# Attention and experts on one core: base loads, a square on GpSimd, and a start by halves

## The chip, the core and the metric

The kernel runs on one core of a Trainium2 chip. A core has four computing engines that run side by side and meet only at semaphores: TensorE (PE in the profile; its weight loads are PEld), VectorE (DVE), ScalarE (ACT) and GpSimd (POOL). SyncE (SP) issues transfers; ScalarE and GpSimd can issue them too. Each engine takes its instructions from a list of its own, in the order of that list. TensorE writes its results to PSUM, from which VectorE and ScalarE take them to SBUF.

The metric is the device time of one execution in microseconds (us): lower is better. Before the change the median of three runs is 3160.34 us, from 3158.16 to 3162.79.

## The reference

The input x is [8, 1024, 512]: 8 batches of 1024 tokens. One layer of attention is followed by one layer of experts, each on a layer norm of its input and with its input added back.

```python
# attention, per head of dh = 32 (16 heads)
theta_q = xh / (1 + |w_q|) + b_q + t * phi_q      # t: position; k alike, v without t
Q = concat(cos(theta_q), sin(theta_q)); K alike; V = cos(theta_v) + sin(theta_v)
out = softmax(causal(Q K^T / sqrt(2 dh))) V
theta_out = out / (1 + |w_out|) + b_out
x = x + cos(theta_out) + sin(theta_out)           # sin, cos by a table of 2048 with interpolation
# experts, E = 8, top 2, at most 160 tokens of a batch for an expert
p = softmax(layernorm(x) @ Wr + br); two best experts of a token, place by order of arrival
y = relu(tokens @ W1 + b1) @ W2 + b2; x = x + sum of p * y over the token's experts that kept it
```

## The kernel before

**Attention.** Work goes in 32 iterations n = 4 b + c: batch b, and a chunk c of four heads. An iteration has two pairs of heads. `scores` makes tiles of Q K^T on TensorE (L688, with the mask by L702) in one of three PSUM tiles (`two_banks`), and ScalarE takes each by an exponential (L708); `attend` multiplies the exponentials with v on TensorE (L722), and VectorE takes the result out of one of two PSUM banks (L730). `turn` transposes it back to tokens (L216) and divides by the sums (L757, L759).

Angles are integers whose wrap-around is the turn. For q and k an iteration adds, on VectorE, the transposed x and a base (the position's part of the angle) in `qk_pre` (L529), and takes the remainder by a shift in `angle` (L442). Interpolation is a polynomial in the low 16 bits: `square` (L446, ScalarE) makes (f / 65536 - 0.5)^2 out of them, `sine` (L449) the sine, and `times` (L452, VectorE) multiplies the two. Eight transfers then spread the features to two `qk` tiles (L613). `o_pre` and `o_post` do the same with the attention's output: bias and angle, then square and sine, then L452 on tile `t_r`, the sum with x (L662) and batch statistics (L665).

Bases of chunks 0 to 3 are made once by `make_base` and stored to DRAM (L501); from n = 4 on `load_base` fetches that of iteration n + 2 as one transfer of 1 MB (L509) into a single buffer, free once L529 of the iteration before has read it.

**The router.** When a batch is complete, its router runs between the next batch's attention. At c = 0 of the next batch (in the text `begin` is set there), the last chunk's output is squared and finished (L1924 and L1925) and the router starts: it is a generator that is advanced at fixed places. Its first step, at c = 1, aggregates the statistics, takes inverse roots and makes rows 0 and 1 of the normalised x (L814, two row buffers); each row tile is stored to DRAM for the experts (L820). TensorE transposes rows (L216) and multiplies them with Wr (L876). At the end of c = 3 slot and token numbers are ready (L978, L983).

Then `scatter` writes them to a slot table in DRAM: 16 indirect transfers by GpSimd per batch (L773), each of which waits for the landing of the one before, since they write the same table. `fetch_slots` (L1006, two transfers by GpSimd) reads the table of a batch back; its place in the text is two batches after that batch. Batches 6 and 7 are scattered in `ending`, beside the first expert.

**The order.** TensorE, ScalarE, VectorE and SP issue their instructions in the order of the text (`manual_schedule`). GpSimd is not in that list: the framework's scheduler places its instructions, by dependencies and its own idea of when they are ready.

**The start.** x of batch 0 is loaded by tiles; statistics (`first_stats`), inverse roots and normalisation (`layernorm_first`, tiles by turns on VectorE and ScalarE), and `qk_first` makes the features of n = 0 by halves of 512 tokens. GpSimd makes the positions (L188), the affine part of two bases (L473) and, ahead of that, the constant columns of two v tiles (L381, L382). ScalarE rounds the base (L483, L486), VectorE scales it (L489).

**The experts** follow with nearly two thirds of the time (L1258, L1372, L1491, L1540) and are not changed.

Of the kernel before, what the change touches and what calls it, by code (L numbers as in the profile page):

```python
# [12 lines left out]
F32 = mybir.dt.float32  # L13
I32 = mybir.dt.int32
U16 = mybir.dt.uint16
BF16 = mybir.dt.bfloat16
AF = mybir.ActivationFunctionType
# [5 lines left out]
P = 128  # L23
# [51 lines left out]
def preln_attn_moe_kernel(  # L75
# [133 lines left out]
    def two_banks():  # L209
        return ps_sc.tile([P, 2, 512], F32, name="ps_s")  # L210
# [7 lines left out]
    def magnitude(t):  # L218

        nc.vector.scalar_tensor_tensor(t, t, -1.0, t, ALU.mult, ALU.max)  # L220
        nc.vector.scalar_tensor_tensor(t, t, 1.0, t, ALU.add, ALU.max)
        nc.vector.reciprocal(t, t)

    def in_units(t):

        nc.vector.scalar_tensor_tensor(t, t, UNITS, t, ALU.mult, ALU.max)
# [9 lines left out]
    def first_stats(t0, t1):  # L236
        for t in range(t0, t1):
            st = small.tile([P, nc.vector.BN_STATS_DIM], F32, name="st")
            nc.vector.bn_stats(st, first_tiles[t])
            nc.vector.bn_aggr(first_mv[:, t, :], st)  # L240
# [15 lines left out]
    nc.tensor.transpose(ps, vec_in, ident[: 6 * NCH, : 6 * NCH])  # L256
    nc.vector.tensor_copy(vecs, ps)

    nc.vector.tensor_copy(inv_qk, vecs[:, : 2 * NCH])
    magnitude(inv_qk)  # L260
    in_units(inv_qk)

    ones = own.tile([P, P], F32, name="ones")
    nc.gpsimd.memset(ones, 1.0)

# [26 lines left out]
    def mask():  # L292
        for part in range(2):
            for a in range(2):
                r = slice(a * 64, (a + 1) * 64)
                nc.gpsimd.tensor_copy(later_b[r, part, :], later[r, 1 + part - a, :])
                nc.gpsimd.tensor_copy(keys_b[r, part, part * 64 : part * 64 + 64], ident[r, r])
# [75 lines left out]
            nc.vector.scalar_tensor_tensor(y, t, 1.5, y, ALU.add, ALU.mult)  # L373
        return y

    v_tiles = []
    for i in range(2):
        vt = vp.tile([P, NTT, HPC, 2 * DH], F32, name=f"v_{i}", tag=f"v_{i}")


        nc.gpsimd.memset(vt[:, :, :, DH:], 0.0)  # L381
        nc.gpsimd.memset(vt[:, :, :, DH : DH + 1], 1.0 / (SUM_UNIT * UNITS))  # L382
        v_tiles.append(vt)

    def load_b1():
        t = own.tile([E * NHC, P], F32, name="vec_in")
# [36 lines left out]
    def layernorm_first():  # L423

        mv = first_mv
        rstd = inverse_root(mv[:, :, 1], "rstd")
        off = small.tile([P, NTT], F32, name="top")
        nc.vector.scalar_tensor_tensor(off, mv[:, :, 0], -1.0, rstd, ALU.mult, ALU.mult)
        for t, xt in enumerate(first_tiles):
            if t % 2:  # L430
                nc.scalar.activation(
                    xt, xt, AF.Identity, bias=off[:, t : t + 1], scale=rstd[:, t : t + 1]
                )
            else:
                nc.vector.tensor_scalar(
                    xt, xt, mv[:, t, 0:1], rstd[:, t : t + 1], ALU.subtract, ALU.mult
                )

    def angle(p, r):
        nc.vector.tensor_scalar(r, p, TURN_SHIFT, None, ALU.logical_shift_left)  # L442

    def square(p):
        f = p.bitcast(U16).rearrange("p (s two) -> p s two", two=2)[:, :, 0]
        nc.scalar.activation(p.bitcast(F32), f, AF.Square, bias=split_c, scale=1.0 / FINE)  # L446

    def sine(r):
        nc.scalar.activation(r.bitcast(F32), r, AF.Sin, scale=STEP_ACT)  # L449
# [7 lines left out]
    def make_base(c):  # L457


        p = (base_first, room[0])[c] if c < 2 else (  # L460
            qkt.tile([P, 2, S], F32, name="qk_base") if c == 2 else room[0]
        )
        r = qkt.tile([P, 2, S], I32, name="qk_r").bitcast(F32) if c == 2 else room[1]
        if c > 1:
            nc.gpsimd.iota(
                p, pattern=[[0, 2], [1, S]], base=0, channel_multiplier=0,
                allow_small_or_imprecise_dtypes=True,
            )
        affine = nc.gpsimd.tensor_scalar if c < 2 else nc.vector.tensor_scalar
        for i in range(2):  # L470
            phi = vecs[:, (4 + i) * NCH + c : (4 + i) * NCH + c + 1]
            bias = vecs[:, (2 + i) * NCH + c : (2 + i) * NCH + c + 1]
            affine(p[:, i, :], p[:, i, :], phi, bias, ALU.mult, ALU.add)  # L473
        if c < 2:
            rs = [r[:, i, :] for i in range(2)]
            if c == 1:

                rs = [
                    ep.tile([P, 2, 512], F32, name="e_512", bufs=8).rearrange("p a n -> p (a n)")
                    for _ in range(2)  # L480
                ]
            for i in range(2):
                nc.scalar.activation(  # L483
                    rs[i], p[:, i, :], AF.Identity, bias=round_c[:, :1], scale=UNITS
                )
                nc.scalar.activation(rs[i], rs[i], AF.Identity, bias=round_c[:, 1:])  # L486
                yield
            for i in range(2):
                nc.vector.scalar_tensor_tensor(  # L489
                    p[:, i, :], p[:, i, :], UNITS, rs[i], ALU.mult, ALU.subtract  # L490
                )
        else:
            nc.vector.tensor_scalar(p, p, UNITS, None, ALU.mult)
            if c == 2:
                yield
                nc.vector.tensor_scalar(r, p, ROUNDT, ROUNDT, ALU.add, ALU.subtract)
                yield
                nc.vector.tensor_tensor(p, p, r, ALU.subtract)
            else:
                wrap(p, r)  # L500
        nc.sync.dma_start(base_d[c], p)  # L501
        bases[c] = p

    def load_base(n):
        if n < NCH:
# [26 lines left out]
                )  # L532
            yield p, r

    def qk_first():


        base = bases.pop(0)
        f, r = (qkt.tile([P, 2, S], I32, name=name) for name in ("qk_f", "qk_r"))
        c = qkt.tile([P, 2, S], F32, name="qk_c")  # L540
        pairs = [qkp.tile([P, 2, S], F32, name="qk") for _ in range(2)]
        halves = [slice(h * 512, (h + 1) * 512) for h in range(2)]
        for h, hs in enumerate(halves):
            ps = two_banks()
            for t in range(4):
                by_halves(ps[:, :, t * 64 : (t + 1) * 64], xn_tiles[0][h][:, t, :P])
            for i in range(2):
                for a in range(2):
                    cols = lambda t: t[:, i, hs].rearrange("p (t a q) -> p t a q", a=2, q=64)[
                        :, :, a, :  # L550
                    ]
                    nc.vector.scalar_tensor_tensor(
                        cols(f), ps[:, a, :256].rearrange("p (t q) -> p t q", q=64),
                        inv_qk[:, i * NCH : i * NCH + 1], cols(base), ALU.mult, ALU.add,
                    )
            angle(f[:, :, hs], r[:, :, hs])
        for hs in halves:
            nc.scalar.activation(c[:, :, hs], r[:, :, hs], AF.Abs)
            nc.scalar.activation(
                c[:, :, hs], c[:, :, hs], AF.Sin, bias=quarter_c, scale=-STEP_ACT  # L560
            )
            for i in range(2):
                square(f[:, i, hs])
            sine(r[:, :, hs])
        v = v_pre(0)
        next(v)
        for hs in halves:
            for i, t in enumerate((c, r.bitcast(F32))):
                times(t[:, :, hs], f[:, :, hs], t[:, :, hs])
                send = (nc.sync, nc.gpsimd)[i].dma_start  # L570
                for pr in range(2):
                    for a in range(2):
                        src = slice((2 * pr + a) * DH, (2 * pr + a + 1) * DH)
                        dst = slice(a * 64 + i * DH, a * 64 + (i + 1) * DH)
                        send(pairs[pr][dst, :, hs], t[src, :, hs])
            v_st = rest(v) or v_st
        return pairs, v_st


# [160 lines left out]
    def rest(gen):  # L740
        got = None
        for got in gen:
            pass
        return got
# [1027 lines left out]
    next(base1)  # L1772
    rest_of_loads()
    mask()
    first_stats(2, NTT)
    layernorm_first()
    rest(base0)
    next(base1)
    pairs, v_st = qk_first()
    sine(v_st[1])  # L1780
    square(v_st[0])
    load_x(1)
# [7 lines left out]
    for n in range(NCK):  # L1790
# [36 lines left out]
            turn(0, halves0, pos)  # L1827
        if more:
            angle(*qk_st)
        if begin or c == 3 and b > 0:  # L1830
            next(route)
        if n and n + 2 < NCK:
            load_base(n + 2)
        if n == 2:
            load_mid(b)
        if late:
# [43 lines left out]
        if late:  # L1880
            turn(1, halves1, pos)
            o_st = o_pre(n - 1, pos)
        if begin:
            square(v_st[0])
        rest(choice)
# [4 lines left out]
        if c == 3 and b > 0:  # L1890
            next(route)
            if b > 1:
                fetch_slots(b - 2)
            if b < B - 1:
                scatter()


        some(3, *products)
# [22 lines left out]
        some(3, *ahead)  # L1921
        begin = c == 0 and late
        if begin or not more:
            square(o_st[0])  # L1924
            rest(o_post(n - 1, o_st))  # L1925
        if begin:
            route = router(b - 1)
# [77 lines left out]
```

## Time and profile before

| | before |
|---|---|
| median of the runs | 3160.34 us |
| profiled execution | 3160.96 us |
| its span, first to last instruction | 3159.2 us |
| busy TensorE, VectorE, ScalarE, GpSimd | 3085.4, 2393.9, 1686.1, 421.3 us |
| scatters (L773) on GpSimd | 128, busy 153.6 us, 280.9 us between them until the one before has landed |
| squares of the output (L446 on `o_p`) | 32, median 1.146 us |
| base loads (L509) | 28, 1 MB, 6.5 us to landing |
| row stores (L820) | 72, 256 KB, 2.4 us to landing |
| VectorE's wait for row stores before L814, 190 to 1240 us | 12.8 us in 10 waits |

A row of the timeline has the start in us from the span's begin, the length in us, the engine, the line, the operation, the tile written and the tiles read (`out<-in`), their shapes, how many equal instructions are put together (x8) and, in brackets, how long the engine stood idle before it and what ended that. An engine with a q is its sequencer: SPq rows are issues of transfers. A group's row has busy time and the mean of one in ns, and then the idle time before its instructions. Busy shares are means over stages, and TensorE's instructions are pipelined with modelled ends.

### The profile page before, as it was taken

How to read it: one execution, taken by the hardware profiler on the slowest of the kernel's cores; microseconds unless marked ns; L12 is line 12 of the kernel's file. 1: busy time of each engine (PE TensorE's matmuls, PEld its weight loads, DVE VectorE, ACT ScalarE, POOL GpSimd, SP SyncE). 2: the span in 40 equal slices, each digit the busy share in tenths (PEclk: the TensorE clock that was granted, in tenths of full speed). 3: DMA queues.
4: the chain of work that ended last, by engine and by line, in shares of the span. 5: the costliest groups of instructions: out<-in, count | busy, mean ns of one | idle time of the engine just before them, and what ended most of it. 6: DMA issues, size and time to landing. Idle time of an engine off the chain costs nothing.

```text
span 3159.2 us, 53457 instructions
## 1 busy us (share of the span) xinstructions
PE 3085.4 (98%) x20422; PEld 2149.6 (68%) x20422; DVE 2393.9 (76%) x4962; ACT 1686.1 (53%) x2672; POOL 421.3 (13%) x387
## 2 busy tenths in 40 slices
PE   5999999999999999999999999999999999999998
PEld 2454444544444544689699699699698698698697
DVE  8888888888888776738678678677777777777775
ACT  7888888888788885413423423423423423423423
POOL 3000202010101122320110110010110010110110
PEclk9999999999999999999999999999999999999999
DMA  5435454544545352433523523523523523423421
GB/s 168 148 101 167 110 165 133 156 135 147 155 140 161 81 168 63 142 84 96 156 52 92 156 50 99 155 50 99 150 54 102 142 57 105 135 57 108 133 46 22
DMA packets 288559, 358.86 MB, mean 114 GB/s; under 512 B 28376, under 2 KB 199088, under 8 KB 276272
## 3 DMA queue, kind: packets, MB, share of 16 engines
q1 hardware_dynamic: 264944, 312.20, 33.4%
q0 software_dynamic: 22912, 43.22, 7.5%
q8 instruction: 162, 2.65, 0.4%
q14 instruction: 93, 0.76, 0.1%
q10 hardware_dynamic: 448, 0.02, 0.0%
HBM read 207.02 MB, written 81.22 MB: 91 GB/s over the span
## 4 chain that ended last, share of the span: by engine, by line
PE 75%; ACT 12%; DVE 7%; DMA 3%; issue 2%; SPq 0%; POOLq 0%; POOL 0%; ACTq 0%; DVEq 0%
PE ps_p L1258 30%; PE ps_p L1491 13%; PE ps_s L688 8%; PE ps_p L1372 8%; PE ps_p L1540 7%; PE av L722 7%; ACT e L708 6%; ACT qk_c L598 1%; DMA xn_d<-xn 1%; ACT t_r L449 1%; PE ps_s L216 1%; ACT qk_r L449 1%; ACT L598 1%; DMA qk<-qk_r 1%; ACT L1908 1%
## 5 line engine op out<-in xcount | busy, mean ns | idle before, releaser
L688 PE MATMUL ps_s<-qk 64*128 64x512 f32 (+3 forms) x3072 | 584.6, 503 | 31.3 <-ACT e L708 13.7
L708 ACT ACTIVATE e<-ps_s 128x1024 f32<-128x1024 f32 (+1 forms) x640 | 554.4, 944 | 73.4 <-PE ps_s L702 45.3
L722 PE MATMUL av<-e,v 128*64 128x512 f32 (+3 forms) x3072 | 509.5, 488 | 0.0
L688 PEld LDWEIGHTS ps_s<-qk 64*128 64x128 f32 x3072 | 261.1, 188 | 219.1 <-ACT e L708 105.9
L722 PEld LDWEIGHTS av<-e,v 128*64 128x64 f32 x3072 | 206.0, 137 | 278.9 <-issue 258.5
L1258 PE MATMUL ps_p<-xe,w 128*128 128x256 f32 (+1 forms) x1024 | 317.6, 433 | 1.1 <-issue 1.1
L1258 PE MATMUL ps_p<-xe_s,t 128*128 128x256 f32 (+1 forms) x1024 | 317.7, 433 | 0.0
L1258 PE MATMUL ps_p<-xe,t 128*128 128x256 f32 (+1 forms) x1024 | 317.7, 433 | 0.0
L1336 POOL DMA_INDIRECT out_dram<-y,slots x80 | 127.6, 1595 | 1237.2 <-ACT y L1331 956.8
L773 POOL DMA_INDIRECT slot_d<-token,slot x128 | 153.6, 1200 | 1026.2 <-issue 627.2
L1258 PEld LDWEIGHTS ps_p<-xe_s,t 128*128 128x128 f32 x1024 | 194.4, 190 | 81.4 <-issue 0.8
L1258 PEld LDWEIGHTS ps_p<-xe,t 128*128 128x128 f32 x1024 | 194.2, 190 | 80.4 <-issue 0.4
L1258 PEld LDWEIGHTS ps_p<-xe,w 128*128 128x128 f32 x1024 | 193.7, 190 | 79.4 <-issue 1.2
L1301 DVE TENSOR_TENSOR hid<-hid 128x256 f32<-128x256 f32 (+1 forms) x128 | 63.5, 496 | 199.3 <-ACT hid L1299 199.1
L1258 PE MATMUL ps_p<-xe_s,w 128*128 128x256 f32 (+1 forms) x512 | 158.9, 433 | 0.6 <-ACT p L1274 0.6
L1372 PE MATMUL ps_p<-w,hid 128*128 128x256 f32 x640 | 142.9, 379 | 0.0
L1491 PE MATMUL ps_p<-w,hid 128*128 128x128 f32 x1104 | 141.8, 275 | 0.0
L702 PEld LDWEIGHTS <-keys_b 64*128 64x128 bf16 x1536 | 78.7, 95 | 91.1 <-issue 72.4
L730 DVE TENSOR_SCALAR av_sb<-av,inv_o 128x512 f32<-128x512 f32 x128 | 94.4, 746 | 57.7 <-PE av L722 57.6
L1491 PEld LDWEIGHTS ps_p<-w,hid 128*128 128x128 f32 x1104 | 135.3, 192 | 1.9
L1372 PEld LDWEIGHTS ps_p<-w,hid 128*128 128x128 f32 x640 | 121.1, 190 | 16.4
L1268 ACT COPY hid<-ps_p 128x256 f32<-128x256 f32 (+1 forms) x128 | 53.9, 421 | 139.4 <-PE ps_p L1258 127.4
(314 smaller groups left out, 5502.3 us busy)
## 6 DMA issues: line engine op xcount, KB each, us to landing
w<-in_L_ffn_W_dram SPq DMA_DIRECT2D x256, 256.0 KB, 3.5
w<-in_L_ffn_W_dram SPq DMA_DIRECT2D x64, 512.0 KB, 6.6
qk<-qk_c SPq DMA_DIRECT2D x124, 256.0 KB, 4.6
qk<-qk_r SPq DMA_DIRECT2D x120, 256.0 KB, 5.2
qk_base<-base_d SPq DMA_DIRECT2D x28, 1024.0 KB, 6.5
xn_d<-xn SPq DMA_DIRECT2D x72, 256.0 KB, 2.4
rows_d<-xg SPq DMA_DIRECT2D x70, 256.0 KB, 2.1
x_mid<-in_L_attn_x_dram SPq DMA_DIRECT2D x16, 1024.0 KB, 9.9
```

Source lines behind the costliest of these rows:

```text
L688: nc.tensor.matmul(ps[:, a, at : at + w], lhsT=pair[r, 1, kb * P : (kb + 1) * P], rhs=pair[r, 0, q0 : q0 + w], start=at == 0, stop=not own ...
L702: nc.tensor.matmul(out_, lhsT=keys_b[r, part, :], rhs=late, start=False, stop=part == 1, skip_group_check=True,)
L708: nc.scalar.activation(e, ps[:, :, :n], AF.Exp, scale=UNIT * UNIT / math.sqrt(2 * DH))
L722: nc.tensor.matmul(av[a * 64 : (a + 1) * 64, q0 - 512 * h :], lhsT=vt[:, kb, 2 * pr + a, :], rhs=es[i][:, a, at : at + w], start=kb == 0, ...
L730: nc.vector.tensor_scalar(av_sb, av, inv_o[:, q : q + 1], None, ALU.mult)
L773: queued = nc.gpsimd.indirect_dma_start(out=slot_d[b], out_offset=bass.IndirectOffsetOnAxis(ap=idx, axis=0), in_=src, in_offset=None,)
L1258: nc.tensor.matmul(ps, lhsT=weights[:, k, :], rhs=rows[:, k, :], start=first and k == 0, stop=last and k == 1, skip_group_check=True,)
L1301: TT(g1, g3, h22, ALU.add)
L1336: ins = nc.gpsimd.indirect_dma_start(out=out, out_offset=bass.IndirectOffsetOnAxis(ap=meta[:, e, jj[r], 0:1], axis=0), in_=y, in_offset=No ...
L1372: nc.tensor.matmul(ps, lhsT=hid[:, k, part, cols], rhs=ws[weight][:, k, :], start=first and k == 0, stop=last and k == NHQ - 1, skip_group ...
L1491: nc.tensor.matmul(ps, lhsT=left[:, k, :], rhs=right[:, k, :], start=first and k == 0, stop=k == 3, skip_group_check=True,)
L1540: nc.tensor.matmul(of(ps, b), lhsT=hid[:, k, part, b * P : (b + 1) * P], rhs=ws[weight][:, k, :], start=first and k == 0, stop=last and k ...
```

## The change

1. In an iteration, `load_base` is called ahead of the router's step instead of behind it. On SP this puts seven base loads (n = 5, 9, ..., 29) ahead of the two row tiles' stores.
2. At c = 0 (n = 4, 8, ..., 28) the square of the batch's last output chunk is `square_beside`, called right after `o_pre`: two GpSimd operations, a scale and shift from the 16-bit view, and a product of the tile with itself. The ScalarE `square` of these seven is left out. `scatter()` is called behind it, where before it was called at the end of c = 3. At n = 4 there is nothing to scatter.
3. The start: the v columns are filled behind the masks; the inverse of 1 + |w| for q and k (`inv_qk`, five small VectorE operations) is taken behind the first statistics; VectorE normalises tiles 0 to 4 and ScalarE 5 to 7; the base of chunk 0 is scaled by halves of positions; both, and the features, go half by half in `qk_first`. The store of base 0 comes behind the features' transfers, and v's first product behind the first half's features.

TensorE's list is the same, VectorE's the same but for the start, and ScalarE's the same but for the seven squares and one normalisation.

```diff
@@ -255,10 +255,6 @@
     ps = two_banks()[:, 0, : 6 * NCH]
     nc.tensor.transpose(ps, vec_in, ident[: 6 * NCH, : 6 * NCH])
     nc.vector.tensor_copy(vecs, ps)
-
-    nc.vector.tensor_copy(inv_qk, vecs[:, : 2 * NCH])
-    magnitude(inv_qk)
-    in_units(inv_qk)
     ones = own.tile([P, P], F32, name="ones")
     nc.gpsimd.memset(ones, 1.0)
@@ -373,14 +369,14 @@
             nc.vector.scalar_tensor_tensor(y, t, 1.5, y, ALU.add, ALU.mult)
         return y
-    v_tiles = []
-    for i in range(2):
-        vt = vp.tile([P, NTT, HPC, 2 * DH], F32, name=f"v_{i}", tag=f"v_{i}")
-
-
-        nc.gpsimd.memset(vt[:, :, :, DH:], 0.0)
-        nc.gpsimd.memset(vt[:, :, :, DH : DH + 1], 1.0 / (SUM_UNIT * UNITS))
-        v_tiles.append(vt)
+    v_tiles = [
+        vp.tile([P, NTT, HPC, 2 * DH], F32, name=f"v_{i}", tag=f"v_{i}") for i in range(2)
+    ]
+
+    def v_columns():
+        for vt in v_tiles:
+            nc.gpsimd.memset(vt[:, :, :, DH:], 0.0)
+            nc.gpsimd.memset(vt[:, :, :, DH : DH + 1], 1.0 / (SUM_UNIT * UNITS))
     def load_b1():
         t = own.tile([E * NHC, P], F32, name="vec_in")
@@ -426,17 +422,22 @@
         rstd = inverse_root(mv[:, :, 1], "rstd")
         off = small.tile([P, NTT], F32, name="top")
         nc.vector.scalar_tensor_tensor(off, mv[:, :, 0], -1.0, rstd, ALU.mult, ALU.mult)
-        for t, xt in enumerate(first_tiles):
-            if t % 2:
-                nc.scalar.activation(
-                    xt, xt, AF.Identity, bias=off[:, t : t + 1], scale=rstd[:, t : t + 1]
-                )
-            else:
-                nc.vector.tensor_scalar(
-                    xt, xt, mv[:, t, 0:1], rstd[:, t : t + 1], ALU.subtract, ALU.mult
-                )
-
-
+
+        def by_vector(t):
+            nc.vector.tensor_scalar(
+                first_tiles[t], first_tiles[t], mv[:, t, 0:1], rstd[:, t : t + 1],
+                ALU.subtract, ALU.mult,
+            )
+
+        for t in range(4):
+            by_vector(t)
+        for t in range(5, NTT):
+            nc.scalar.activation(
+                first_tiles[t], first_tiles[t], AF.Identity, bias=off[:, t : t + 1],
+                scale=rstd[:, t : t + 1],
+            )
+        yield
+        by_vector(4)
     def angle(p, r):
         nc.vector.tensor_scalar(r, p, TURN_SHIFT, None, ALU.logical_shift_left)
@@ -444,6 +445,12 @@
     def square(p):
         f = p.bitcast(U16).rearrange("p (s two) -> p s two", two=2)[:, :, 0]
         nc.scalar.activation(p.bitcast(F32), f, AF.Square, bias=split_c, scale=1.0 / FINE)
+
+    def square_beside(p):
+        f = p.bitcast(U16).rearrange("p (s two) -> p s two", two=2)[:, :, 0]
+        t = p.bitcast(F32)
+        nc.gpsimd.tensor_scalar(t, f, 1.0 / FINE, -0.5, ALU.mult, ALU.add)
+        nc.gpsimd.tensor_tensor(t, t, t, ALU.mult)
     def sine(r):
         nc.scalar.activation(r.bitcast(F32), r, AF.Sin, scale=STEP_ACT)
@@ -466,6 +473,7 @@
                 p, pattern=[[0, 2], [1, S]], base=0, channel_multiplier=0,
                 allow_small_or_imprecise_dtypes=True,
             )
+        bases[c] = p
         affine = nc.gpsimd.tensor_scalar if c < 2 else nc.vector.tensor_scalar
         for i in range(2):
             phi = vecs[:, (4 + i) * NCH + c : (4 + i) * NCH + c + 1]
@@ -485,7 +493,14 @@
                 )
                 nc.scalar.activation(rs[i], rs[i], AF.Identity, bias=round_c[:, 1:])
                 yield
-            for i in range(2):
+            if c == 0:
+                for h in range(2):
+                    hs = slice(h * 512, (h + 1) * 512)
+                    nc.vector.scalar_tensor_tensor(
+                        p[:, :, hs], p[:, :, hs], UNITS, r[:, :, hs], ALU.mult, ALU.subtract
+                    )
+                    yield
+            for i in range(2 if c else 0):
                 nc.vector.scalar_tensor_tensor(
                     p[:, i, :], p[:, i, :], UNITS, rs[i], ALU.mult, ALU.subtract
                 )
@@ -499,7 +514,6 @@
             else:
                 wrap(p, r)
         nc.sync.dma_start(base_d[c], p)
-        bases[c] = p
     def load_base(n):
         if n < NCH:
@@ -532,8 +546,9 @@
                 )
             yield p, r
-    def qk_first():
-
+    def qk_first(base0, base1):
+
+        normal = layernorm_first()
         base = bases.pop(0)
         f, r = (qkt.tile([P, 2, S], I32, name=name) for name in ("qk_f", "qk_r"))
@@ -541,6 +556,10 @@
         pairs = [qkp.tile([P, 2, S], F32, name="qk") for _ in range(2)]
         halves = [slice(h * 512, (h + 1) * 512) for h in range(2)]
         for h, hs in enumerate(halves):
+            next(normal, None)
+            next(base0)
+            if not h:
+                next(base1)
             ps = two_banks()
             for t in range(4):
                 by_halves(ps[:, :, t * 64 : (t + 1) * 64], xn_tiles[0][h][:, t, :P])
@@ -563,7 +582,6 @@
                 square(f[:, i, hs])
             sine(r[:, :, hs])
         v = v_pre(0)
-        next(v)
         for hs in halves:
             for i, t in enumerate((c, r.bitcast(F32))):
                 times(t[:, :, hs], f[:, :, hs], t[:, :, hs])
@@ -574,6 +592,7 @@
                         dst = slice(a * 64 + i * DH, a * 64 + (i + 1) * DH)
                         send(pairs[pr][dst, :, hs], t[src, :, hs])
             v_st = rest(v) or v_st
+        rest(base0)
         return pairs, v_st
@@ -1772,11 +1791,12 @@
     next(base1)
     rest_of_loads()
     mask()
+    v_columns()
     first_stats(2, NTT)
-    layernorm_first()
-    rest(base0)
-    next(base1)
-    pairs, v_st = qk_first()
+    nc.vector.tensor_copy(inv_qk, vecs[:, : 2 * NCH])
+    magnitude(inv_qk)
+    in_units(inv_qk)
+    pairs, v_st = qk_first(base0, base1)
     sine(v_st[1])
     square(v_st[0])
     load_x(1)
@@ -1827,10 +1847,10 @@
             turn(0, halves0, pos)
         if more:
             angle(*qk_st)
+        if n and n + 2 < NCK:
+            load_base(n + 2)
         if begin or c == 3 and b > 0:
             next(route)
-        if n and n + 2 < NCK:
-            load_base(n + 2)
         if n == 2:
             load_mid(b)
         if late:
@@ -1880,6 +1900,9 @@
         if late:
             turn(1, halves1, pos)
             o_st = o_pre(n - 1, pos)
+            if c == 0:
+                square_beside(o_st[0])
+                scatter()
         if begin:
             square(v_st[0])
         rest(choice)
@@ -1891,8 +1914,6 @@
             next(route)
             if b > 1:
                 fetch_slots(b - 2)
-            if b < B - 1:
-                scatter()
         some(3, *products)
@@ -1921,7 +1942,8 @@
         some(3, *ahead)
         begin = c == 0 and late
         if begin or not more:
-            square(o_st[0])
+            if not begin:
+                square(o_st[0])
             rest(o_post(n - 1, o_st))
         if begin:
             route = router(b - 1)
```

## The prediction

> **What bounds the kernel now.** First the page's busy shares: TensorE is the bound, in attention (the first 15 slices) as much as in the experts.
>
> ```profile
> PE 3085.4 (98%) x20422; PEld 2149.6 (68%) x20422; DVE 2393.9 (76%) x4962; ACT 1686.1 (53%) x2672; POOL 421.3 (13%) x387
> PE   5999999999999999999999999999999999999998
> ```
>
> So a gain must come out of TensorE's few waits, and anything that keeps TensorE waiting is lost whole. The view of waits, TensorE alone, lists them: behind the start, 13.7 us for ScalarE's exponentials (L708), 4.0 for VectorE's `lg` (L881), 2.6 for the router's rows (L814).
>
> Then I read one begin, that of n = 8 (c = 0), engine by engine in the timeline. GpSimd, from the scatters of batch 0 on (start, length, what):
>
> ```profile
> 317.53 2.97 POOL L773 DMA_INDIRECT slot_d<-token,slot  x1 [264.53 <-issue]
> ...
> 358.44 0.96 POOL L773 DMA_INDIRECT slot_d<-token,slot  x1 [2.87 <-DMA slot_d<-token,slot]
> ...
> 371.52 0.96 POOL L773 DMA_INDIRECT slot_d<-token,slot  x1 [1.42 <-DMA slot_d<-token,slot]
> 373.90 1.57 POOL L1006 DMA_DIRECT2D slots<-slot_d  x2 [1.43 <-DMA slot_d<-token,slot]
> 375.47 0.20 POOL L980 IOTA token<- 128x16 int32 x1
> ```
>
> Each of the 16 scatters waits for the landing of the one before, so they hold GpSimd's queue for 56 us. Behind them stands L1006, which the text issues three iterations later, at n = 11: GpSimd's list is not in the order of the text. VectorE around the same begin:
>
> ```profile
> 351.20 0.69 DVE L442 TENSOR_SCALAR t_r<-o_p 128x1024 int32<-128x1024 int32 x1
> ...
> 355.33 2.28 DVE L452 SCALAR_TENSOR_TENSOR qk_r<-qk_f,qk_r 128x2048 f32<-128x2048 f32 x1
> 358.97 1.23 DVE L452 SCALAR_TENSOR_TENSOR t_r<-o_p,t_r 128x1024 f32<-128x1024 f32 x1 [1.36 <-ACT o_p L446]
> ...
> 364.31 2.72 DVE L529 SCALAR_TENSOR_TENSOR qk_f<-ps_s,inv_qk,qk_base 128x512 int32<-128x512 f32 x4 [1.18 <-PE ps_s L216]
> ...
> 372.42 1.00 DVE L814 TENSOR_SCALAR xn<-x_mid,mv,rstd 128x512 f32<-128x512 f32 x2
> ```
>
> The square is what L452 on `t_r` waits for; its input is ready at 351.9. From L529 to the rows (L814) VectorE has no gap. And TensorE:
>
> ```profile
> 365.11 7.96 PE L722 MATMUL av<-e,v 128*64 128x512 f32 x48
> 373.00 1.13 PE L688 MATMUL ps_s<-qk 64*128 64x512 f32 x4
> 373.97 0.25 PE L702 MATMUL ps_s<-later_b,keys_b 64*128 64x64 bf16 x4
> 374.05 0.67 PE L216 MATMUL ps_s<-ident,xn 64*128 64x64 f32 x16
> ```
>
> At 374.05 it transposes the router's rows, 0.63 us after L814 has made them: VectorE has next to no lead here.
>
> **The change part by part.** *The square by GpSimd.* Seven ScalarE squares of 1.15 us go (L446, n = 4, 8, ..., 28). Each holds back an exponential for which TensorE waits 0.45 us: at most 3.2 us in all. In their place come seven pairs on GpSimd. What the pairs stand behind is read from the built program of the changed kernel, by GpSimd's list (lines of the changed file):
>
> ```
> 43 L452 TensorScalarPtr o_p<-o_p 128x1024
> 44 L453 TensorTensor o_p<-o_p 128x1024
> 45 L792 DMACopy slot_d_62<-token,slot 3328x2 x16
> 46 L1025 DMACopy slots<-slot_d_62 128x8x2
> 47 L1025 DMACopy slots<-slot_d_62 32x8x2
> 48 L999 Iota token 128x16
> 49 L452 TensorScalarPtr o_p<-o_p 128x1024
> ```
>
> The first pair is n = 4's, with no scatters pending. The next is n = 8's, and the 16 scatters of batch 0, their two fetches and an iota stand ahead of it. The text puts them behind, but the scatters' inputs are ready at 316.7 (slot and token, before the end of n = 7), the square's at 351.9, and the list has them in that order for all six batches 0 to 5. The first scatter's wait names the same VectorE instruction as before, so they still start near 317.5. VectorE's order around it is unchanged: L452 on `t_r` waits for GpSimd, and everything behind it waits too: batch statistics, the next features (L529), the rows, all evictions of attention (L730).
>
> How late is it? From the start of the fetches to VectorE: fetches 1.57, iota 0.20, first operation 1.19 (row of L473, the same size), second operation, and 0.3 for hand-overs. The second has two inputs; nearest is L1233, 256 elements:
>
> ```profile
> L1233 POOL TENSOR_TENSOR t<-w,t 128x256 f32<-128x256 f32 x12 | 10.0, 833 | 0.4
> L473 POOL TENSOR_SCALAR qk_base<-qk_base,vecs 128x1024 f32<-128x1024 f32 x2 | 2.4, 1197 | 0.6 <-DVE vecs L257 0.6
> ```
>
> Bounds are 0.83 us (no growth with size) and 3.3 (four times). I take 3.0: the row less 0.1 of fixed cost (L193's smallest memset is 0.09), times four. That makes 6.3 us in all. The Trainium skill (GPSIMD Engine Reference, section 3.1 Elementwise) has 4497 ns for 2048 elements; an estimate from it, half of that, is 2.25 us, and the sum would be 4.5 us smaller.
>
> The fetches start at 373.90, 529.42, 679.04, 826.87, 992.07 and 1132.32 in the six batches. In four of them the last scatters collide with the router's row stores (issued 523.76, 674.90, 825.18, 981.31), which will come later than they; at the undisturbed 2.38 us from issue to the next step, the fetches start at 373.9, 526.1, 676.7, 826.2, 986.0 and 1132.3. L452 on `t_r` starts now at 358.97, 509.73, 660.88, 811.15, 967.22 and 1116.97. With 6.3 added it is late by 21.2, 22.7, 22.1, 21.4, 25.1 and 21.6: sum 134.
>
> What covers it? TensorE goes on with the transposes of L529's input, two attends (L722) and one score tile, and stops at 374.05 for rows that come 21 us late. Cover is the 1.18 us that VectorE waits before L529 and the 0.63 of lead: 1.8 each. Stall: 134 - 11 = **123 us**. After it, TensorE is the bound again and nothing gives the time back.
>
> TensorE also slows after idling. It waits 3.7 us up to 62.18; then:
>
> ```profile
> 34.00:62.00 28.00, 24.28 (x164) 12.96 (x164) 23.83 (x25) 24.71 (x24) 5.83 (x6) 0.99 0.59 199
> 62.00:70.00 8.00, 7.82 (x26) 3.96 (x28) 5.48 (x6) 5.65 (x8) 0.00 (x0) 0.61 0.99 230
> ...
> 836.00:840.00 4.00, 4.00 (x34) 1.25 (x32) 1.08 (x4) 2.05 (x2) 0.00 (x0) 0.57 0.06 25
> ```
>
> (columns: stretch, length, busy of PE, PEld, DVE, ACT, POOL, granted clock, DMA share, GB/s). A mean of 0.61 over 8 us is half clock for 6.2, and 0.57 over 4 us for 3.4: 1.7 to 3.1 us lost after each of the six stalls. I take 2.5, **15 us**.
>
> The scatters' spacing could also change while VectorE stands. From 366.79 to 373.90 they run at 2.38 us with VectorE busy throughout; the wider steps before (358.44 to 366.79) fall beside the feature transfers that SP issues from 354.81 on, and these stay. So I keep the rows' spacing. At 2.38 from the twelfth scatter on, this batch's fetches would start at 370.3, and the six batches would be 19 us shorter in all: the low end. The Trainium skill, SBUF — State Buffer, section SBUF: two separate sides, says that a DMA issued by GpSimd lacks its descriptors while VectorE runs two-port operations; by it a standing VectorE would free the scatters, and the sum would be at that low end.
>
> *Base load ahead of the row stores* (SP, n = 5, 9, ..., 29). It waits for L529, issues some 7 us earlier (now 374.12, at L529's end 366.95), and its 1 MB no longer stands ahead of the rows 2 and 3, for which VectorE's L814 waits (view of waits: 12.8 us in 10 waits). TensorE's share is L881's 4.0 and L814's 2.6. Gain between 0 and 6.6; I take 3, since TensorE's wait at 379.81 is only 0.41 in this batch.
>
> *The head.* Five small operations (L259 to L226, 8.11 to 10.65) move behind the statistics: the statistics start 2.5 us earlier and the five, 0.9 in a quiet place, come behind them, so the root starts 1.6 us earlier. The first half is then ready after four normalisations (1.9), half a base (1.2), four L552 (1.65) and the angle (0.7): 2.6 us earlier than 24.64, the second half about 0.9 earlier than 26.94. First scores wait for the first half's transfer (34.06), ScalarE's exponentials soon for the second. Between 0.7 and 2.6; the base's store is moved on SP behind eight feature transfers and now stands just ahead of the load of x (L171), whose rows are normalised from n = 1 on, so nothing waits there. I take 1.5. The memsets of v (1.83 + 0.28) move behind the casts near 17 and end near 19, before the first attends after 45 read them: nothing. n = 4's square gains up to 0.5.
>
> Sum: 123 + 15 - 3 - 1.5 - 0.5 = 133 us. The profiled execution took 3160.96 us (span 3159.2), 0.6 above the median of 3160.34: **3294 us**.
>
> **The rivals.** *A, the squares are not held up* (the change does what its text says): TensorE regains 3.2 + 3 + 1.5, about 7.7 us, 3153. For it: GpSimd is 13% busy, and at n = 4 it holds. Against: the built list, and L1006's place in the trace. It decides only if the pair runs ahead of the scatters, or their fetches start by 354.5 (358.97 + 1.8 - 6.3); the row has 373.90. Chance 0.04.
>
> *B, half of the stall is covered*, if TensorE has other work queued: about 60 us, 3220. For it: two engines have slack. Against: TensorE's list is fixed and the next entry at 374.05 needs the rows. 0.07.
>
> *C, the stall costs more*, each restart at half clock for longer, or features late a second time: 5 us more per batch, above 3320. For it: the half-clock row; against: VectorE and TensorE are late by the same amount. 0.05.
>
> **How the numbers follow.** The forecast has 0.84. Its bounds: down, second operation at 0.83 (-13), clock 1.7 (-5), scatters at 2.38 (-19), together 3257; up, fetches as late as now (+12), clock 3.1 (+4), no gains (+5), 3315. Range 3256 to 3318. A measurement here tells about 0.2% (6.3 us) from no change: faster only A (0.03 of its 0.04), same 0.01, slower 0.96.
>
> **What would show it.** Right: VectorE's L452 on `t_r` waiting for POOL by about 20 us at six begins and not at n = 4, TensorE idle as long before the rows' transposes, half clock behind it, GpSimd's pair after the fetches. Wrong: the pair before the scatters, or six waits under 10 us. Base part: L814 no longer waits for row stores of rows 2 and 3. Head: first scores at 32 to 33.4 rather than 34.06.

## The result: 3.1% slower, and the profile after

The changed kernel takes 3259.86 us in the median of six runs (3257.99 to 3262.82), the kernel before, beside it, 3161.57 (3158.16 to 3163.36): a ratio of 1.0313, 95% interval 1.0301 to 1.0324. The forecast was 3294 in a range of 3256 to 3318, so the direction and the mechanism are right and the size is a third too large: 133 us were forecast, 98 came, and the time is 4 us above the low end of the range. The profiled execution took 3261.03 us, its span 3259.3, which is 100.1 more than the span of before; all sums below are made against these two spans.

TensorE's row of busy shares, first for the span, then in 40 slices, of the changed kernel:

```profile
PE 3091.3 (95%) x20422; PEld 2159.9 (66%) x20422; DVE 2390.0 (73%) x4963; ACT 1679.2 (52%) x2664; POOL 433.3 (13%) x401
PE   5999797979798998999999999999999999999998
```

98% has become 95%, and six slices in the attention have a 7 or an 8 where before there was a 9: the loss is in six places, not spread out. The view of waits, TensorE alone, of the changed kernel (us in total, times, longest):

```profile
PE ps_s L216 <- DVE xn L833: 104.7, 6, 19.6
PE ps_s L216 <- DVE xn L427: 15.6, 2, 11.8
PE ps_s L707 <- ACT e L727: 10.3, 10, 3.7
PE ps_s L707 <- DMA qk<-qk_r: 8.6, 1, 8.6
```

The first row is new (2.6 us before): six stalls ahead of the transposes of the router's rows. What VectorE waited for, in the same view of VectorE:

```profile
DVE t_r L459 <- POOL o_p L453: 123.7, 7, 22.2
```

L459 is the line that was L452, L453 the second operation of GpSimd's pair. Of the seven waits one, at n = 4, is 1.78 us; the six others are 22.18, 19.45, 20.23, 21.67, 19.74 and 18.60 (start of L459 less the end of the instruction before it), in sum 121.9. The timeline of the begin of n = 8, GpSimd:

```profile
354.98 0.97 POOL L792 DMA_INDIRECT slot_d<-token,slot  x1 [2.86 <-DMA slot_d<-token,slot]
359.37 0.97 POOL L792 DMA_INDIRECT slot_d<-token,slot  x1 [3.42 <-DMA slot_d<-token,slot]
364.34 0.97 POOL L792 DMA_INDIRECT slot_d<-token,slot  x1 [4.00 <-DMA slot_d<-token,slot]
...
369.09 0.97 POOL L792 DMA_INDIRECT slot_d<-token,slot  x1 [1.42 <-DMA slot_d<-token,slot]
371.48 1.60 POOL L1025 DMA_DIRECT2D slots<-slot_d  x2 [1.43 <-DMA slot_d<-token,slot]
373.07 0.21 POOL L999 IOTA token<- 128x16 int32 x1
373.22 1.08 POOL L452 TENSOR_SCALAR o_p<-o_p 128x1024 f32<-128x1024 uint16 x1
374.39 1.89 POOL L453 TENSOR_TENSOR o_p<-o_p 128x1024 f32<-128x1024 f32 x1
```

The pair runs last, behind the scatters, the fetches and the iota, as the built list had it. VectorE and TensorE at the same place:

```profile
351.85 2.28 DVE L459 SCALAR_TENSOR_TENSOR qk_r<-qk_f,qk_r 128x2048 f32<-128x2048 f32 x1
376.32 1.23 DVE L459 SCALAR_TENSOR_TENSOR t_r<-o_p,t_r 128x1024 f32<-128x1024 f32 x1 [22.18 <-POOL o_p L453]
...
388.48 1.00 DVE L833 TENSOR_SCALAR xn<-x_mid,mv,rstd 128x512 f32<-128x512 f32 x2
```

```profile
369.32 0.25 PE L721 MATMUL ps_s<-later_b,keys_b 64*128 64x64 bf16 x4
389.17 1.11 PE L216 MATMUL ps_s<-ident,xn 64*128 64x64 f32 x16 [19.60 <-DVE xn L833]
...
395.81 0.64 PE L895 MATMUL ps_s<-xT,wr_sb 128*32 128x256 f32 x8
```

VectorE stands from 354.13 to 376.32, then needs its usual 12 us to the rows, and TensorE, with nothing else in its list, stands 19.60 us. The clock behind the stall, by stretches (start and end, length, busy of PE, PEld, DVE, ACT, POOL, granted clock, DMA share, GB/s):

```profile
369.50:389.00 19.50, 0.07 (x4) 0.00 (x0) 12.17 (x39) 3.84 (x4) 5.28 (x6) 0.62 0.18 55
389.00:392.00 3.00, 2.83 (x27) 2.26 (x29) 3.00 (x7) 1.15 (x2) 0.00 (x0) 0.50 0.46 175
392.00:396.00 4.00, 4.00 (x26) 2.07 (x26) 2.04 (x3) 2.49 (x3) 0.00 (x0) 0.67 0.35 131
396.00:400.00 4.00, 4.00 (x58) 1.85 (x52) 1.97 (x4) 2.83 (x4) 0.00 (x0) 1.00 0.03 6
```

Half clock until some 5.5 us after the restart, as forecast in kind.

The 100.1 us add up from the two profiles: the stalls at the rows, 104.7 for 2.6, are +102.1; TensorE's busy time, 3091.3 for 3085.4, +5.9; the waits for ScalarE's exponentials, 10.3 for 13.7, -3.4; for `lg`, 0.8 for 4.0, -3.2; the first scores' transfer, 8.6 for 12.4, -3.8; the first normalisations, 15.6 for 13.8, +1.8. That is 99.4; smaller waits make up the rest.

### The profile page after: what moved, and what is told of

Read it like the earlier page. It is cut to its first block, busy times and chain, and to the rows that moved or that the text cites. A ratio compares the mean times of both kernels' runs of the same rounds, so it can differ in the third digit from the quotient of the medians.

```text
span 3259.3 us, 53482 instructions
## 1 busy us (share of the span) xinstructions
PE 3091.3 (95%) x20422; PEld 2159.9 (66%) x20422; DVE 2390.0 (73%) x4963; ACT 1679.2 (52%) x2664; POOL 433.3 (13%) x401
## 4 chain that ended last, share of the span: by engine, by line
PE 67%; DMA 10%; DVE 9%; issue 7%; ACT 4%; POOL 1%; SPq 1%; POOLq 0%; DVEq 0%; ACTq 0%
PE ps_p L1277 29%; PE ps_p L1510 13%; DMA slot_d<-token,slot 8%; PE ps_p L1391 7%; PE ps_p L1559 6%; PE ps_s L707 5%; PE av L741 4%; ACT e L727 3%; PE ps_s L216 1%; DMA qk<-qk_r 1%; DVE st_mid L684 1%; DVE qk_f L543 1%; DMA xn<-in_L_attn_x_dram 0%; POOL o_p L453 0%; DVE x_mid L681 0%
## 5 line engine op out<-in xcount | busy, mean ns | idle before, releaser
L707 PE MATMUL ps_s<-qk 64*128 64x512 f32 (+3 forms) x3072 | 589.3, 507 | 21.4 <-ACT e L727 10.3
L707 PEld LDWEIGHTS ps_s<-qk 64*128 64x128 f32 x3072 | 268.4, 192 | 206.3 <-ACT e L727 94.4
L792 POOL DMA_INDIRECT slot_d<-token,slot x128 | 140.9, 1101 | 958.8 <-DVE token L1002 675.6
L447 ACT ACTIVATE qk_f<-qk_f,split_c 128x1024 f32<-128x1024 uint16 (+1 forms) x66 | 70.5, 1115 | 218.2 <-DVE qk_r L443 218.2
L216 PE MATMUL ps_s<-ident,xn 64*128 64x64 f32 x976 | 46.2, 236 | 121.7 <-DVE xn L833 104.7
L1510 PE MATMUL ps_p<-w,hid 128*128 128x128 f32 x1104 | 141.9, 275 | 0.0
L1510 PEld LDWEIGHTS ps_p<-w,hid 128*128 128x128 f32 x1104 | 135.3, 192 | 1.9
```

Of the source, the lines that this page charges most:

```text
L216: nc.tensor.transpose(turned[:, a, :], src[r, :], ident[r, r])
L707: nc.tensor.matmul(ps[:, a, at : at + w], lhsT=pair[r, 1, kb * P : (kb + 1) * P], rhs=pair[r, 0, q0 : q0 + w], start=at == 0, stop=not own ...
L792: queued = nc.gpsimd.indirect_dma_start(out=slot_d[b], out_offset=bass.IndirectOffsetOnAxis(ap=idx, axis=0), in_=src, in_offset=None,)
L1510: nc.tensor.matmul(ps, lhsT=left[:, k, :], rhs=right[:, k, :], start=first and k == 0, stop=k == 3, skip_group_check=True,)
```

## The experiments

The theory: the pair costs nothing by being on GpSimd; it costs what stands ahead of it in GpSimd's queue. The rivals: a square on GpSimd is too slow wherever it stands; or the scatters' new place, the base loads or the head make the loss. Ratios are against runs of the kernel before on the same chip (medians 3161.57 for the change, 3157.95, 3160.76 and 3159.53 us for the other three sets).

| run | median us | ratio (95%) | TensorE's stalls at the rows, us |
|---|---|---|---|
| the change as it is | 3259.86 | 1.0313 (1.0301 to 1.0324) | 104.7 |
| square back on ScalarE | 3152.0 | 0.9982 (0.9972 to 0.9991) | 0.7 |
| square on GpSimd alone | 3260.56 | 1.0327 (1.0313 to 1.0341) | 103.6 |
| all, pair first | 3147.52 | 0.9959 (0.9946 to 0.9973) | 1.0 |
| all, fourteen scatters ahead | 3206.45 | 1.0150 (1.0134 to 1.0166) | 46.2 |
| three operations more, one step each | 3313.11 | 1.0496 (1.0480 to 1.0512) | 155.4 |
| three operations more, two steps each | 3282.11 | 1.0388 (1.0371 to 1.0405) | 123.1 |
| base loads alone | 3156.07 | 0.9985 (0.9976 to 0.9994) | under 0.7 |
| head alone | 3158.64 | 0.9990 (0.9981 to 0.9999) | 2.5 |
| pair first, without base and head | 3158.14 | 0.9987 (0.9978 to 0.9996) | 2.6 |

**The square back on ScalarE.**

```diff
             if c == 0:
-                square_beside(o_st[0])
                 scatter()
...
-            if not begin:
-                square(o_st[0])
+            square(o_st[0])
```

> The changed kernel with one thing undone: a batch's last square is ScalarE's again, after the rows, and the scatters, the base loads and the head stay as changed. Theory (the two GpSimd operations standing behind sixteen scatters are the whole loss): VectorE's wait for GpSimd at the six begins (121.9 us) and TensorE's six stalls (104.7 us) go, what is left is the gain of the base loads and of the head, about -3 and -2.8 us, so 3153 to 3159 us, 0.1 to 0.3% under the kernel before. Rival (the scatters' new place, beside the feature transfers, holds the rows up by itself): stalls of 15 us and more stay before the rows' transposes and the time stays at 3240 to 3260 us.

3152.0 us, 0.18% under the kernel before and a microsecond under the theory's bracket. The whole loss hangs on the pair; the scatters' place in the text, the bases and the head hold nothing up.

**The square on GpSimd alone.** The kernel before, with `square_beside` after `o_pre` and the ScalarE square left out at c = 0; the scatters stay at the end of c = 3.

> The kernel before with one thing done: GpSimd squares a batch's last features, the scatters are asked for where they were, and in the instruction list as built the two operations then stand ahead of the sixteen scatters of their begin. Theory (the order on GpSimd's queue is the cause, not GpSimd's speed): the pair takes about 7 us beside a busy VectorE, as at n = 4 of the changed kernel (3.20 and 3.80 us), VectorE waits up to 2 us more at a begin, and the time is 3158 to 3172 us. Rival (a square on GpSimd is too slow wherever it stands): the six stalls stay, 3240 to 3262 us.

3260.56 us, the changed kernel's time, and its stalls:

```profile
PE ps_s L216 <- DVE xn L820: 103.6, 6, 19.2
```

The number falls in the rival's bracket, but my expectation was wrong in its premise, so it doesn't decide for the rival. In GpSimd's list the pair of n = 8 doesn't stand ahead: the list opens with the pair of n = 4, has the scatters of batch 0 next and the pair of n = 8 behind them, just as in the changed kernel:

```profile
372.38 1.60 POOL L1012 DMA_DIRECT2D slots<-slot_d  x2 [1.43 <-DMA slot_d<-token,slot]
373.97 0.21 POOL L986 IOTA token<- 128x16 int32 x1
374.12 1.09 POOL L451 TENSOR_SCALAR o_p<-o_p 128x1024 f32<-128x1024 uint16 x1
375.29 1.89 POOL L452 TENSOR_TENSOR o_p<-o_p 128x1024 f32<-128x1024 f32 x1
```

So the run doesn't tell order from speed. It tells something else: where the text calls `scatter`, ahead of the square or behind it, makes no difference, because GpSimd's list comes out the same. Order is tested by the next run.

**All parts, the pair first.** The scatters of a begin are held behind the pair's second operation, which `square_beside` now returns, by an order in the queue.

```diff
...
+    def scatter(count=2 * NTT * TOPK, late=False, behind=None):
...
-            if late:
+            if late or behind is not None:
                 tc.add_manual_dep(
-                    ins, mixed[-1].name,
+                    ins, (mixed[-1] if late else behind).name,
...
-                square_beside(o_st[0])
-                scatter()
+                squared = square_beside(o_st[0])
+                scatter(behind=squared)
```

> The changed kernel with the order that its text has: the scatters of a begin are held behind the second of the two GpSimd operations, by an order in the queue and no other wait. All parts of the change are in. Theory (the order is the cause): no stall before the rows' transposes, the pair at 5 to 7 us as at n = 4, VectorE waiting 1 to 2 us for it, and the base loads' and the head's gain left over: 3152 to 3166 us. Rival (the loss is in GpSimd's speed or in what the scatters share with the feature transfers): 3200 us or more.

3147.52 us, 0.41% under the kernel before and a little better than the theory's bracket. Same instructions, same engines as in the changed kernel: the order of one queue is worth 112 us. This is also the fastest of all the versions here. Its timeline at the begin of n = 8, GpSimd and then VectorE:

```profile
348.83 1.05 POOL L452 TENSOR_SCALAR o_p<-o_p 128x1024 f32<-128x1024 uint16 x1 [141.82 <-DVE t_r L443]
349.96 3.81 POOL L453 TENSOR_TENSOR o_p<-o_p 128x1024 f32<-128x1024 f32 x1
353.94 2.96 POOL L792 DMA_INDIRECT slot_d<-token,slot  x1 [0.18 <-issue]
360.73 0.99 POOL L792 DMA_INDIRECT slot_d<-token,slot  x1 [3.83 <-DMA slot_d<-token,slot]
```

```profile
349.24 2.77 DVE L459 SCALAR_TENSOR_TENSOR qk_c<-qk_f,qk_c 128x2048 f32<-128x2048 f32 x1
351.94 0.74 DVE L749 TENSOR_SCALAR av_sb<-av,inv_o 128x512 f32<-128x512 f32 x1
352.60 3.31 DVE L459 SCALAR_TENSOR_TENSOR qk_r<-qk_f,qk_r 128x2048 f32<-128x2048 f32 x1
355.84 1.21 DVE L459 SCALAR_TENSOR_TENSOR t_r<-o_p,t_r 128x1024 f32<-128x1024 f32 x1
```

L459 on `t_r` starts without a wait. The scatters start 40 us later than in the changed kernel, and no wait for them shows.

**Fourteen scatters ahead, two behind.** A graded test from the other side: as the run before, with `scatter(NTT * TOPK - 2)` between the square and `scatter(behind=squared)`.

> The kernel in which the pair stands first, with fourteen of a begin's sixteen scatters let ahead of the pair and two, and the fetch, behind it. In the changed kernel's trace the fourteenth scatter was issued 10.2, 6.5, 5.4, 9.4, 5.3 and 5.1 us after VectorE was ready (six begins); with 0.97 us for its issue and 3.1 us for the pair VectorE would wait 14.3, 10.6, 9.4, 13.5, 9.4 and 9.1, in sum 66 us, TensorE 17 less (as 121.9 against 104.7): 49 us. Theory (the wait is the scatters' and the fetch's own times, one behind the other): 3147.5 and 49 and 2 for the half clock, 3190 to 3206 us. Rival (what counts is the fetch and its wait, or that the pair stands behind any scatter): as the kernel in which the pair stands first (3145 to 3152), or as the changed kernel (3258 to 3263).

VectorE waited 9.3, 10.6, 9.3, 14.2, 9.4 and 10.7 us, in sum 63.4 where 66 were worked out; TensorE:

```profile
PE ps_s L216 <- DVE xn L833: 46.2, 6, 11.4
```

46.2 for 49. The profiled span is 3200.3 us, 52.3 above that of the kernel with the pair first; the median, 3206.45, is just above the upper end. Two scatters and the fetch behind them, taken out of the way, are worth half the loss. The wait is the queue's own times, one behind the other.

**Three operations more in the pair**, for n > 4.

```diff
+        for _ in range(more):
+            nc.gpsimd.tensor_scalar(t, t, 1.0, None, ALU.mult)
```

> The changed kernel with three more multiplications by 1.0 of 128x1024 elements in place between the two GpSimd operations, in the six begins after n = 4. Each took 1.07 to 1.10 us at such a place, so the pair's end is 3.3 us later. Theory (TensorE's stall is what is left of the pair's lateness, nothing more covers it): the six stalls grow by 3.3 us each, the time by 19 to 20 us, to 3277 to 3281 us. Rival (another transfer or engine ends the stall just behind the pair): 3258 to 3268 us.

3313.11 us: neither theory's number. The group's row tells why (busy us, mean ns of one):

```profile
L454 POOL TENSOR_SCALAR o_p<-o_p 128x1024 f32<-128x1024 f32 x18 | 49.9, 2771 | 1.5
```

The eighteen took 2.77 us each, not 1.08: 49.9 us. VectorE's wait grew by 50.4 (174.1 for 123.7), TensorE's stalls by 50.7. The stall follows the pair one to one; the price of an operation was wrong. That price was tried by itself, with the two steps that the pair's first operation has:

```diff
-            nc.gpsimd.tensor_scalar(t, t, 1.0, None, ALU.mult)
+            nc.gpsimd.tensor_scalar(t, t, 1.0, 0.0, ALU.mult, ALU.add)
```

> As the run with three more operations between the two of the pair, but each written as the pair's first one is: a multiplication by 1.0 and an addition of 0.0 in one instruction, where that run had the multiplication alone and took 2.77 us for one instead of 1.08. Theory (the form of the operation set that price; the stall follows VectorE's wait one to one): 1.1 to 1.2 us for one, as in the pair's first and in the bases' affine part before (1.20), six stalls longer by 3.4 us each, 3277 to 3284 us. Rival (the 32-bit input of the tile sets it): 2.8 us for one and 3308 to 3318 us again.

```profile
L454 POOL TENSOR_SCALAR o_p<-o_p 128x1024 f32<-128x1024 f32 x18 | 18.8, 1044 | 1.5
```

Same tile, same type, 1.04 us each. 18.8 us were added, the wait grew by 18.2 (141.9), the stalls by 18.4. The form sets the price, and the stall follows the wait one to one a second time.

**The other two parts, each alone.** The base load ahead of the router's step, in the kernel before:

> The kernel before with one thing done: a base's load is asked for ahead of the row stores on SyncE's queue. Theory (the rows' later halves wait for the first halves' stores, which the load held up): VectorE's waits at rows for a store shrink from 16.2 us in 12 to some 5 us, TensorE's waits for rows and logits (2.6 and 4.0 us) by 3 to 5 us, the time by 2 to 4 us against the kernel before of the same runs. Rival (those waits are covered, or the base's transfer takes its bandwidth from the rows all the same): within 1 us of the kernel before.

The ratio 0.9985 is -4.7 us (-1.9 to -7.6), a little more than the 2 to 4 expected. VectorE's waits at rows for a row store are 8.0 us in 7 where they were 16.2 in 12, and TensorE's wait at the router's rows is under 0.7 for 2.6; VectorE's row:

```profile
DVE xn L814 <- DMA xn_d<-xn: 8.0, 7, 1.8
```

The head, in the kernel before:

> The kernel before with the changes at its head alone: normalisation, base and first features by halves, the memory sets of v's columns and the three small operations on the units later. Theory (the first scores start 1.8 us and the first feature wait ends 2.8 us sooner, and nothing later gives it back): 2 to 3 us under the kernel before. Rival (ScalarE's wait of the first blocks takes it back): within 1 us.

First scores start at 32.35 us for 34.06. The ratio 0.9990 is -3.2 us (-0.3 to -6.0). In the profiled execution the evictions of attention are 1.9 us ahead of those of before up to n = 8 and only 0.3 ahead at the end of attention; but the run with base loads alone, whose head is that of before, was ahead by 1.7 us at the same early place, so single profiles don't resolve this part. The runs do, barely.

**Pair first, without base and head.**

> The kernel before with GpSimd's square and, behind it in the queue, the scatters, but its own base loads and head. It tells what the square and the scatters are worth in the order that the text has. Theory (with the pair first VectorE's wait of 1.4 us at each begin for ScalarE's square goes, and ScalarE has seven squares of 128x1024 less): 2 to 6 us under the kernel before of the same runs. Rival (the gain of the kernel with the pair first is the base loads' and the head's alone): within 1 us of the kernel before.

0.9987, -4.1 us (-1.3 to -7.0): the square on GpSimd, in the right order, is a gain of its own. VectorE's seven waits of some 1.4 us for ScalarE go. The three parts by themselves, -4.7, -3.2 and -4.1, sum to -12.0; all together with the pair first gave -13 (0.9959 of 3157.95).

## Why the prediction was right, and where its sizes were off

*The order in GpSimd's list* was the deciding step, and it held: six begins, not n = 4, the pair behind fetches and iota. The pair-first run shows it to be the cause.

*The tail, 6.3 us from the fetches to VectorE,* was 4.84 in the changed kernel's six begins (371.48 to 376.32 at n = 8): 8.8 us of the sum too many. The term that was mis-sized is the second operation, taken as 3.0 by stretching a row of 256 elements; it took 1.89, which is 6.7 of the 8.8. The Trainium skill's figure (GPSIMD Engine Reference, section 3.1 Elementwise; half of its 4497 ns is 2.25 us, an estimate) was nearer; the measured 1.89 holds while VectorE stands. Both figures, 3.0 and 2.25, and the measured one lie within the bounds given.

*The scatters' end* was worked out from the rows of before with the row stores taken out. In the changed kernel the sixteenth scatter started 15.0, 12.2, 13.0, 14.2, 12.5 and 10.0 us after VectorE was ready; before it was 13.9, 15.3, 14.9, 13.9, 19.8 and 14.8. Together with the waits for ScalarE that go (8.5 us), lateness against before came to 113.4, not 134: 8.8 of the difference is the tail, 11.8 the scatters' earlier end. What I had missed lies 40 us earlier, at the first scatter. That of batch 1 took 3.01 us before and the next came 6.3 later; in the changed kernel 1.09 and 2.5, so the chain is a step ahead. Over the six batches this first step came to 17.3 us where it was 37.8. It goes with the pair in GpSimd's list, not with the scatters' place in the text: the same scatter took 3.00 us with the square back on ScalarE and 1.09 with the square on GpSimd alone. Why it starts a little sooner there, 0.3 us behind its token (L1002) instead of 0.8, stays open, and so does how much of the 11.8 is due to it.

*Cover of 1.8 each* was nearly right: 113.4 of lateness gave 104.7 of stall, 1.5 each.

*Half clock, 15 us,* was nearly right at the restarts. From the restart to the first product with Wr (L895) TensorE ran the same instructions without a gap in 6.64, 6.16, 5.53, 6.15, 6.68 and 5.45 us; in the kernel before they took 4.06 to 4.14, at n = 8 from 374.05 to

```profile
378.12 0.64 PE L876 MATMUL ps_s<-xT,wr_sb 128*32 128x256 f32 x8
```

That is 1.3 to 2.6 us lost at a restart where 2.5 was taken, 12.1 in all. TensorE's busy time rose by only 5.9 us against the kernel before, because elsewhere it fell: it is 4.8 less than before in the run with ScalarE's square (3080.6), which has the base loads and the head but no stalls. The sum had no term for that, and where it comes from wasn't followed up.

*ScalarE's seven squares, 3.2 at most,* had been left out of the sum beside the stall. TensorE's waits for exponentials did fall by 3.4 us, from 13.7, but that this is the squares' doing isn't shown: they are 12.1 with the squares back on ScalarE, 12.9 with the pair first and nothing else changed. *Base and head, 3 and 1.5:* alone they measured 4.7 and 3.2, and both forecasts lie within those runs' intervals. The head's first scores came at 32.26 us in the changed kernel, as forecast; the base part's sign held only in part, as VectorE still waited 4.7 us in 4 at the rows for a row store (8.0 in 7 with base loads alone). *n = 4's square, a gain of 0.5:* VectorE waited 1.78 us instead of 1.36, 0.4 more.

In one line: 133 forecast, less 20.9 for the stalls (8.8 tail, 11.8 scatters, 2.6 that stood at the rows already, against 2.3 of cover that wasn't there), less 9.1 for TensorE's busy time (2.9 at the restarts, 6.2 elsewhere), less 2.9 for gains taken too small, is 100.1. All of these but the cover moved the time down, to just inside the range: the order was foreseen, but that the number is inside owes something to the range's width.

*The rivals.* A, squares not held up, is what the pair-first kernel is; its price, -7.7, was too small against the -13 measured. B's other work for TensorE did not exist. C did not come.

*Standing VectorE frees the scatters?* The prediction took it from the Trainium skill (SBUF — State Buffer, section SBUF: two separate sides) that they might then come faster. At that place it made no difference: with VectorE standing the steps at n = 8 were 4.4, 5.0, 2.4, 2.4 and 2.4 us, the issues 0.97; before, with VectorE busy, 3.9, 4.5, 3.9, 2.4 and 2.4, the issues 0.96 to 1.03. There was no long issue to free there, and the rest of a step is the wait for the landing. That VectorE can hold up an issue is seen elsewhere (last section).

## What to carry to other kernels

An instruction moved to an idle engine must be looked up in that engine's list as built: a share of 13% busy says nothing of a queue whose entries wait for landings, 16 in a row, and the place in the text may not be the place in the list. If the order is right the same move is a gain; where a scheduler orders the queue, state the order as a dependency. And price an operation from the same form at the same size, with what its neighbour engine does beside it.

## What the runs showed of the hardware that I had not expected

**GpSimd and VectorE take turns.** The pair took 1.08 and 1.89 us while VectorE stood, and 1.05 and 3.81 with the pair first, where VectorE's L459 took 2.77 and 3.31 us instead of 2.28. At n = 4 of the changed kernel:

```profile
199.26 3.20 POOL L452 TENSOR_SCALAR o_p<-o_p 128x1024 f32<-128x1024 uint16 x1 [144.37 <-DVE t_r L443]
202.54 3.80 POOL L453 TENSOR_TENSOR o_p<-o_p 128x1024 f32<-128x1024 f32 x1
```

```profile
199.27 2.28 DVE L459 SCALAR_TENSOR_TENSOR qk_c<-qk_f,qk_c 128x2048 f32<-128x2048 f32 x1
...
202.13 2.46 DVE L459 SCALAR_TENSOR_TENSOR qk_r<-qk_f,qk_r 128x2048 f32<-128x2048 f32 x1
```

The first two start 0.01 us apart, so which came first isn't resolved. If GpSimd's operation waits for the end of VectorE's and then takes its time alone, the first ends at 201.55 + 1.08 = 202.63 (measured 202.46), the second at 204.59 + 1.89 = 206.48 (206.34). In the pair-first run the second would end at 352.01 + 1.89 = 353.90 (353.77), and VectorE's next L459, held until then, at 353.77 + 2.28 = 356.05 (355.91). So here they exclude each other, they don't share. The Trainium skill (SBUF — State Buffer, section Who interferes with whom) has this as an exclusive lock between a VectorE instruction with two SBUF inputs and a GpSimd instruction that reads SBUF, where the later one waits; the four ends agree within 0.2 us.

**The issue of an indirect transfer is held up as well.** Batch 1's first scatter in the kernel before, and VectorE at the same place:

```profile
468.14 3.01 POOL L773 DMA_INDIRECT slot_d<-token,slot  x1 [92.48 <-issue]
```

```profile
467.94 2.28 DVE L452 SCALAR_TENSOR_TENSOR qk_c<-qk_f,qk_c 128x2048 f32<-128x2048 f32 x1
```

The scatter started 0.2 us into an L452 that ended at 470.22, and ended at 471.15: 0.93 after it, as long as an undisturbed issue (0.96). All six first scatters of that kernel are like this: 2.97 to 3.01 us, ended 0.91 to 0.97 after the L452 in which they started. In the changed kernel the same scatters started 0.27 to 0.28 us ahead of that instruction and took 1.08 to 1.13.

**A GpSimd operation with a scalar took 2.77 us with one step and 1.04 with two**, on the same 128x1024 tile in place. Why isn't known from these runs.
